# Context values computed in groups of 128 rows and carried to their batches, with two edits at the start of the second attention

## The chip, the core and the metric

The kernel runs as one program on one core of a Trainium2 chip. The core has TensorE (PE in the profile; its weight loads are listed apart as PEld), VectorE (DVE), ScalarE (ACT), GpSimd (POOL) and SyncE (SP). SP does no arithmetic here: it issues transfers, which the DMA engines carry out. The metric is the time of one execution in device microseconds (us). The median of three executions before the change is 1793.78 us (1792.69 to 1799.24).

## The reference, cut to what matters

The reference is a block of four layers on `x` of shape (16, 256, 256), with a context `ctx` of shape (16, 77, 256). Each layer adds a gated result to `x`:

```python
x = x + tanh(g_xattn[0]) * L0_xattn(ctx, layernorm(x), ...)   # attention over context and latents
x = x + tanh(g_ffn[0])   * L0_ffn(layernorm(x), ...)          # 8 experts, the best two of each token
x = x + tanh(g_xattn[1]) * L1_xattn(layernorm(x), ctx, ctx, fside, mask, ...)
x = x + tanh(g_ffn[1])   * L1_ffn(layernorm(x), ...)          # gated linear attention
```

The change is in the third layer and the work that prepares it. That layer is an attention with 16 heads of 16 columns over the 77 context rows of each batch:

```python
q = heads(query @ wq + wq_b); k = heads(ctx @ wk + wk_b); v = heads(ctx @ wv + wv_b)
attn = softmax(q k^T / 4 + mask) * group_prob
out  = merge(attn @ v) @ wo + wo_b
```

Keys and values depend on the context alone, so they can be computed ahead of the layer.

## The kernel before, in words

The kernel works through stages: stage 0 is the first attention, stage 1 the experts, stage 2 the second attention, stage 3 the gated linear attention. Instructions of PE, ACT, DVE and POOL are mostly issued through a wrapper that keeps them in the order of the program on their engine. The profile therefore gives line 50 (the wrapper) for nearly all of them, and one reads by the names of tiles. SP's transfers are not pinned: a scheduler orders them when the program is built, so a load that needs nothing can stand far ahead of the line that asks for it. The built program gives the transfers of SP eight semaphores in turn; a transfer that reuses one first waits for the transfer eight places before it.

Stage 1 (`stage1_fast`) has sixteen blocks of rows: eight experts for each of two halves of the batches. A block is 640 rows. `fetch` loads a block into one of three `xin` buffers, `turned` transposes it on PE by units of up to 256 rows, `expert` multiplies, copies to one of two `y` buffers on DVE, and writes back to `rows_out`. There are 24 units in each half. `route.next_gather` makes POOL gather 128 rows of a half's results and add them to `x` of a batch; there are 32 gathers for each half, and a gather can begin only when the half's writes have landed.

Between the two halves of stage 1 stands the context work, the main object of the change. Until then the context, already transposed, has been loaded by `load` into four tiles `cT0` to `cT3` of four batches each. The loop over the 16 batches calls `context(b)`. For every fourth batch it first computes the keys of four batches (`context_keys`, tile `kd`): PE forms them in two banks of PSUM and ACT copies them out, twice each, with a mask. Then it computes the values of the batch: two products on PE with the 77 context rows as the stationary operand, and one addition of the bias on DVE into the batch's own tile `vc{b}`, where rows lie in partitions 0 to 76. The banks for this come from a shared pool of four that go round in order. From the seventh batch on, the loop also issues ten gathers.

In the second half of stage 1 a table `steps` sets small jobs between the units: normalization of the first batches for the second attention (`prep.stats`, `prep.norm`, `prep.turn`, `prep.queries`), and at unit `half + 20` the job `prep.spread(0)`. `spread(b)` is two POOL copies that put the columns of `vc{b}` into a tile `vd`, even heads in one half and odd heads in the other. There are three `vd` tiles, used in turn.

Stage 2 (`stage2_fast`) takes one batch after another, each in two halves of the heads, c = 0 and 1. `scores` computes scores into a PSUM tile that has a single buffer, then one exponential on ACT makes `e` from all 2048 columns. For c = 0 ACT then copies the batch's `group_prob` tile into a bank (`gpx`). `weigh` multiplies `e` by it on DVE, giving `pg`; for c = 0 in two calls of 1024 columns. `values` multiplies `pg` with `vd`, and `e` with a matrix of ones (`own`) for the denominators, both into the bank `o`. `outputs` divides. PE's order for batch 0 is: scores (0, 0), queries of batch 1, scores (0, 1), values (0, 0), scores (1, 0), and so on. POOL's order in each batch is two gathers, four small operations for a later batch's normalization, one gather, and then `spread` of the next batch.

Beside the results the kernel keeps flags: the exponentials leave their sums in columns of a tile `most`, whose maximum is tested at the end.

Of the kernel before, what the change touches and what calls it, by code (L numbers as in the profile page):

```python
# [17 lines left out]
P = 128  # L18
# [36 lines left out]
def flamingo_kernel(tc: tile.TileContext, t, out):  # L55


    nc = tc.nc
    with tc.tile_pool(name="flag", bufs=1) as fp:
        check = {n: fp.tile(shape, F32, tag=n, name=n) for n, shape in (  # L60
            ("esum", [P, 2 * S]), ("rsum", [P, S]), ("most", [P, 2 * B]), ("uneven", [P, B]),
            ("gates", [P, 2 * B]), ("second", [P, 16]), ("logs", [P, 2 * B]),
            ("rows", [P, 2, 8]), ("rsum2", [P, 2 * B]), ("rsum0", [P, 4 * B]))}
        for x in check.values():
            nc.gpsimd.memset(x, 0.0)
        bad = check["bad"] = fp.tile([1, 1], I32, tag="bad", name="bad")
        layers(tc, t, out, check)
        with tc.If(nc.values_load(bad[0:1, 0:1], min_val=0, max_val=P,
                                  skip_runtime_bounds_check_because="a count of partitions") > 0):
            layers(tc, t, out, None)  # L70
# [3 lines left out]
def layers(ctx: ExitStack, tc: tile.TileContext, t, out, check):  # L74
# [39 lines left out]
    def c_count(j):  # L114
        return min(P, c_rows - P * j)

    def c_pieces(b):

        lo, hi = b * S2, (b + 1) * S2
        return [(j, max(lo, P * j) - P * j, max(lo, P * j) - lo, min(hi, P * j + P) - max(lo, P * j))  # L120
                for j in range(lo // P, (hi - 1) // P + 1)]
# [968 lines left out]
    def stage1_fast(keep, prep, bank):  # L1090
        with ExitStack() as sx:
# [11 lines left out]
            kb = w1.tile([P, 2, 2], F32, tag="kb", name="kb")  # L1103
            dve.tensor_tensor(kb, bc(vec[:, V_KB:V_KB + 2], [P, 2, 2], 2), bc(pmask, [P, 2, 2], 1), ALU.mult)

            mks, cTs = {}, {}

            def load(b):
                mks[b] = w3_.tile([S2, S], I32, tag="mk", name="mk")
                nc.sync.dma_start(out=mks[b], in_=t["maskT"][b])  # L1110
                if b % 4 == 0:
                    cTs[b // 4] = w1.tile([P, 2, 4, S2], F32, tag=f"cT{b // 4}", name=f"cT{b // 4}")
                nc.sync.dma_start(out=cTs[b // 4][:, :, b % 4, :],
                                  in_=t["ctxT"][b].rearrange("(k p) s -> p k s", p=P))

            def mask(b):

# [10 lines left out]

            def context_keys(q):

                cT = cTs[q]
                kds[q] = keep.tile([P, 2, 2, 4 * S2], F32, tag=f"kd{q}", name=f"kd{q}")
                for c in range(2):
                    ps = bank("k")
                    for k in range(2):
                        pe.matmul(ps[:, :4 * S2], wk2[:, k, c * P:(c + 1) * P],
                                  cT[:, k].rearrange("p b s -> p (b s)"), start=k == 0, stop=k == 1)
                    for h in range(2):
                        act.activation(kds[q][:, c, h, :], ps[:, :4 * S2], AF.Identity,
                                       bias=kb[:, c, h:h + 1], scale=pmask[:, h:h + 1])  # L1140

            def context(b):

                if b % 4 == 0:
                    context_keys(b // 4)
                ps, cT = bank("v"), cTs[b // 4][:, :, b % 4, :]
                for k in range(2):
                    pe.matmul(ps[:S2, :D], cT[:, k, :], wv2[:, k, :], start=k == 0, stop=k == 1)
                vc = keep.tile([S2, D], F32, tag=f"vc{b}", name=f"vc{b}")
                dve.tensor_tensor(vc, ps[:S2, :D], bv[:S2], ALU.add)  # L1150
                ctx_side[b] = negs[b], kds[b // 4][:, :, :, b % 4 * S2:(b % 4 + 1) * S2], vc


            tiles = ROWS // P
# [7 lines left out]
            def fetch(x):  # L1162
                xin[x] = w3_.tile([P, tiles, D], F32, tag="xin", name="xin")
                nc.sync.dma_start(out=xin[x], in_=by_expert(route.rows[x // 8], x % 8))
# [36 lines left out]
            def weigh_rows(n):  # L1201
                if n == 0:
# [7 lines left out]
                     12: [(weigh_rows, 2)],  # L1210
                     half + 6: [(prep.stats, 0)], half + 10: [(prep.norm, 0)], half + 11: [(prep.stats, 1)], half + 12: [(add_bias, 0)],
                     half + 13: [(prep.turn, 0)], half + 15: [(prep.norm, 1)], half + 16: [(prep.stats, 2)], half + 18: [(add_bias, 1)],
                     half + 17: [(prep.queries, 0)], half + 19: [(prep.turn, 1)], half + 20: [(prep.spread, 0)]}
            for n in range(4):
                steps.setdefault(2 + n, []).append((route.scatter, last - 1, n))
                steps.setdefault(13 + n, []).append((route.scatter, last, n))
# [19 lines left out]
            fetch(1)  # L1236
            units(0, half)

            for b in range(B):
                context(b)  # L1240
                if b % 4 == 2 and b < 8:
                    fetch(8 + b // 4)
                if b >= 6:
                    route.next_gather()
            units(half, 2 * half)


# [45 lines left out]
    def stage2_fast(prep, bank, begin):  # L1293
        with ExitStack() as sx:
# [13 lines left out]
            def scores(b, c):  # L1308

                neg, kd, _ = ctx_side[b]  # L1310
                qT = prep.qT[b]
                sc = psc.tile([P, 4, 2, S], F32, tag="sc", name="sc")
                for h in range(2):
                    for g in range(4):
                        r = slice(32 * g, 32 * g + 32)
                        pe.matmul(sc[:S2, g, h, :], kd[r, c, h, :], qT[r, c, :], start=True, stop=True)
                e = es[b, c] = w2e.tile([S2, 4, 2, S], F32, tag="e", name="e")
                act.activation(e, sc[:S2], AF.Exp, bias=neg, accum_out=most[:S2, 2 * b + c:2 * b + c + 1])
                if c == 0:

                    gpx[b] = bank("gpx")
                    act.copy(gpx[b][:S2, :S], gps.pop(b))
# [40 lines left out]
            def run(f, b, *a):  # L1363
                if 0 <= b < B:
                    f(b, *a)

            load(0)
            for b in range(B + 1):
                def early(*batches):
                    if b in batches:  # L1370
                        next(begin)

                run(load, b + 1)
                run(scores, b, 0)
                early(B - 1)
                if b > 0:
                    run(prep.turn, b + 1)
                else:
                    prep.queries(1)
                run(values, b - 1, 1)  # L1380
                run(weigh, b, 0, 0, 2)
                run(outputs, b - 1, 1)
                run(weigh, b, 0, 2, 4)
                early(B - 2, B)
                route.next_gather()
                run(scores, b, 1)
                if b > 0:
                    run(prep.queries, b + 1)
                run(prep.norm, b + 2)
                early(B - 1)  # L1390
                run(weigh, b, 1, 0, 4)
                run(project, b - 1)
                early(B - 2, B - 1)
                route.next_gather()
                run(values, b, 0)
                run(outputs, b, 0)
                run(prep.stats, b + 3)
                early(B - 3, B - 1)
                route.next_gather()
                run(prep.spread, b + 1)  # L1400
                if 2 <= b:
                    load_weights(1)
# [883 lines left out]
```

## Time and profile before

The profile shows one execution in detail; its own time is near, but not equal to, the median.

| what | value |
|---|---|
| median of three executions | 1793.78 us (1792.69 to 1799.24) |
| the profiled execution, its time | 1796.44 us |
| the profiled execution, its span | 1794.6 us |
| context work on PE | 981.8 to 1003.9 us from the start of the span |
| one pair of value products on PE | 0.86 us, 16 pairs |
| one addition into `vc` on DVE | 0.42 us, 16 of them |
| second half of the experts | 1003.9 to about 1051.5 us |
| first scores of the second attention | 1051.67 us |
| first product with `vd` | 1058.69 us |
| two copies of `spread` on POOL | 1.11 us |

All times inside the span count from its start. A timeline row gives the start, the duration of a merged group, the engine, the line, the operation with "written tile <- read tiles", and in brackets the idle time before it with what the profile takes to be its cause. A cause named there is inferred; where the named work was long done, it was another. Rows of "SPq" are issues of transfers, not the transfers themselves. A row of stretches gives a window, its length, then the busy time (and number of instructions) of PE, PEld, DVE, ACT and POOL, the clock granted to TensorE as a share, the busy share of the DMA engines and their GB/s.

### The profile page before, as it was taken

What the parts mean: (1) busy time and instruction counts of PE and PEld (TensorE: products, weight loads), DVE (VectorE), ACT (ScalarE), POOL (GpSimd) and SP (SyncE); (2) the same over time, 40 slices, a digit from 0 to 9 for tenths busy, and PEclk for the clock granted to TensorE, in tenths of its full rate; (3) what the DMA queues carried; (4) which work ended last, traced back from release to release, by engine and by line L of the source; (5) the groups of instructions that cost most, each with busy time, mean ns of one, the idle gap of its engine ahead of it and who ended that gap; (6) DMA issues with size and microseconds to landing.
All of it is one profiled execution on the core that took longest, in us unless ns stands there. A gap on an engine that the chain in (4) does not pass through costs nothing.

```text
span 1794.6 us, 35307 instructions
## 1 busy us (share of the span) xinstructions
PE 1764.7 (98%) x13804; PEld 1225.2 (68%) x13804; DVE 1186.2 (66%) x2713; ACT 856.7 (48%) x1762; POOL 1020.6 (57%) x1002
## 2 busy tenths in 40 slices
PE   8999999999999999999999999999999999999998
PEld 5666666667666666667677766666777777777776
DVE  3345665666666666665556348887777778777875
ACT  4433444434434344334443358775456546545643
POOL 3655676576656776576752676612455545545543
PEclk9999999999999999999999999999999999999999
DMA  9800010000100010000027962300112211211211
GB/s 306 239 1 23 13 39 11 28 20 13 32 29 17 15 36 10 29 24 17 13 96 232 284 151 46 51 8 19 35 35 48 41 41 35 52 41 35 44 40 32
DMA packets 121624, 102.30 MB, mean 57 GB/s; under 512 B 53051, under 2 KB 106979, under 8 KB 120937
## 3 DMA queue, kind: packets, MB, share of 16 engines
q1 hardware_dynamic: 109161, 83.17, 16.3%
q0 software_dynamic: 12288, 16.79, 4.7%
q8 instruction: 111, 1.82, 0.4%
q14 instruction: 64, 0.52, 0.1%
HBM read 56.26 MB, written 38.44 MB: 53 GB/s over the span
## 4 chain that ended last, share of the span: by engine, by line
PE 81%; DVE 9%; POOL 7%; issue 1%; DMA 1%; ACT 0%; POOLq 0%; SPq 0%; DVEq 0%; ACTq 0%
PE o L50 12%; PE qk L50 11%; PE v L50 9%; PE sc L50 8%; PE proj L50 8%; PE kq L1641 5%; PE sc L1641 5%; POOL es L50 4%; PE v L1641 3%; PE proj L1641 3%; PE ex L50 3%; PE gq L1641 2%; PE o L1641 2%; DVE at L50 2%; PE q L50 2%; POOL rs L50 2%
## 5 line engine op out<-in xcount | busy, mean ns | idle before, releaser
L50 POOL TENSOR_SCALAR rs<-mv 128x2 f32<-128x2 f32 (+2 forms) x85 | 16.3, 192 | 367.6 <-DVE mv L50 363.9
L50 DVE RECIPROCAL rd<-o 128x256 f32<-128x256 f32 x64 | 112.3, 1755 | 164.0 <-PE o L50 123.6
L50 POOL TENSOR_TENSOR at<-at,at 128x768 f32<-128x768 f32 x63 | 114.3, 1814 | 151.5 <-DVE at L50 151.5
L50 ACT ACTIVATE e<-sc 128x1024 f32<-128x1024 f32 (+1 forms) x192 | 181.7, 1016 | 18.5 <-PE sc L50 18.5
L50 PE MATMUL sc<-qk 64*128 64x256 f32 (+1 forms) x1536 | 183.1, 384 | 0.5 <-DVE qk L50 0.5
L50 PE MATMUL o<-e,v 128*32 128x256 f32 (+1 forms) x3072 | 177.9, 379 | 0.0
L50 PEld LDWEIGHTS sc<-qk 64*128 64x128 f32 (+1 forms) x1536 | 132.0, 172 | 55.1 <-issue 26.8
L50 POOL TENSOR_TENSOR esum<-esum,es 128x512 f32<-128x512 f32 x128 | 163.5, 1277 | 10.0
L50 PE MATMUL qk<-kvT,wkv 128*128 128x333 f32 x512 | 164.3, 443 | 0.0
L50 ACT ACTIVATE qk<-qk 128x256 f32<-128x256 f32 x128 | 48.8, 382 | 231.4 <-PE qk L50 231.4
L50 POOL TENSOR_TENSOR es<-e 128x1024 f32<-128x1024 f32 x64 | 151.3, 2363 | 12.1 <-ACT e L50 9.0
L50 POOL TENSOR_TENSOR es<-es,e 77x1024 f32<-77x1024 f32 x64 | 150.4, 2350 | 5.0
L50 PEld LDWEIGHTS o<-e,v 128*32 128x32 f32 (+1 forms) x3072 | 99.9, 110 | 66.3
L50 PE MATMUL qk<-kvT,wq 128*128 128x256 f32 x512 | 134.6, 385 | 0.0
L50 DVE COPY qk<-qk 128x333 f32<-128x333 f32 x128 | 64.6, 504 | 93.8 <-ACT qk L50 92.8
L50 POOL DMA_INDIRECT x<-rows_out,pos x64 | 101.4, 1584 | 35.9 <-issue 15.7
L50 PEld LDWEIGHTS qk<-kvT,wq 128*128 128x128 f32 x512 | 94.3, 189 | 35.2 <-issue 9.6
L50 PEld LDWEIGHTS qk<-kvT,wkv 128*128 128x128 f32 x512 | 97.2, 190 | 30.0
L50 PE MATMUL proj<-wo0h,oT 128*128 128x256 f32 x512 | 113.7, 380 | 0.3 <-DVE oT L50 0.3
L50 PE MATMUL v<-wkv,kvT 128*128 128x512 f32 x256 | 113.1, 595 | 0.0
L50 PEld LDWEIGHTS proj<-wo0h,oT 128*128 128x128 f32 x512 | 95.9, 190 | 13.9 <-issue 0.8
L50 POOL DMA_INDIRECT rows<-xw,pos x64 | 66.8, 1043 | 58.5 <-DMA rows<-xw,pos 26.6
(258 smaller groups left out, 3927.9 us busy)
## 6 DMA issues: line engine op xcount, KB each, us to landing
rows<-zero SPq DMA_DIRECT2D x16, 640.0 KB
xin<-rows SPq DMA_DIRECT2D x16, 640.0 KB
r<-rms SPq DMA_DIRECT2D x30, 256.0 KB
rows_out<-y SPq DMA_DIRECT2D x16, 384.0 KB
v<-vctx SPq DMA_DIRECT2D x15, 308.0 KB
x<-in_x_dram SPq DMA_DIRECT2D x16, 256.0 KB
rows_out<-y SPq DMA_DIRECT2D x16, 256.0 KB
rows<-picks SPq DMA_DIRECT2D x16, 256.0 KB
```

Of the source, the lines that this page charges most:

```text
L50: x = getattr(self.engine, name)(*a, **k)
L1641: tc.keep_in_program_order(nc.tensor.matmul(*a, **k))
```

## The change

There are three edits.

1. The values of the context are computed for groups of 128 consecutive context rows, without regard to batches. All 16 x 77 = 1232 rows lie in one tile `cT`; there are ten groups, the last of 80 rows. For each group PE makes two products and DVE one addition, into a tile `vg` of a pool of three buffers (the one that also held the mask tiles). `context_rows(j)` then issues transfers on SP that copy the rows of group j to the tiles `vc{b}` of the batches they belong to, into partitions 0 to 76. There are 25 of them, since a group begins and ends in the middle of batches. `context_rows(j - 1)` is called after the products of group j. The gathers of this loop are one in each turn; there are ten as before. Keys are computed as before, ahead of groups 0, 2, 4 and 6.
2. `prep.spread(0)` moves from unit `half + 20` to unit `half + 2`.
3. For batch 0 and c = 0 alone, ACT copies `group_prob` before the exponential, and the exponential is done in two halves of 1024 columns, with the matching half of `weigh` called after each. The calls of `weigh(0, 0, ...)` in the loop of stage 2 go away for batch 0. The flag tile `most` has one more column, for the sum of the second half.

```diff
-            ("esum", [P, 2 * S]), ("rsum", [P, S]), ("most", [P, 2 * B]), ("uneven", [P, B]),
+            ("esum", [P, 2 * S]), ("rsum", [P, S]), ("most", [P, 2 * B + 1]), ("uneven", [P, B]),
...
-                if b % 4 == 0:
-                    cTs[b // 4] = w1.tile([P, 2, 4, S2], F32, tag=f"cT{b // 4}", name=f"cT{b // 4}")
-                nc.sync.dma_start(out=cTs[b // 4][:, :, b % 4, :],
-                                  in_=t["ctxT"][b].rearrange("(k p) s -> p k s", p=P))
+                nc.sync.dma_start(out=cT[:, :, b * S2:(b + 1) * S2], in_=t["ctxT"][b].rearrange("(k p) s -> p k s", p=P))
...
-            def context(b):
-
-                if b % 4 == 0:
-                    context_keys(b // 4)
-                ps, cT = bank("v"), cTs[b // 4][:, :, b % 4, :]
+            def context_values(j):
+                n, ps = c_count(j), bank("v")
                 for k in range(2):
-                    pe.matmul(ps[:S2, :D], cT[:, k, :], wv2[:, k, :], start=k == 0, stop=k == 1)
-                vc = keep.tile([S2, D], F32, tag=f"vc{b}", name=f"vc{b}")
-                dve.tensor_tensor(vc, ps[:S2, :D], bv[:S2], ALU.add)
-                ctx_side[b] = negs[b], kds[b // 4][:, :, :, b % 4 * S2:(b % 4 + 1) * S2], vc
+                    pe.matmul(ps[:n, :D], cT[:, k, j * P:j * P + n], wv2[:, k, :], start=k == 0, stop=k == 1)
+                vcs[j] = w3_.tile([P, D], F32, tag="mk", name="vg")
+                dve.tensor_tensor(vcs[j][:n], ps[:n, :D], bv[:n], ALU.add)
+
+            def context_rows(j):
+                x = vcs.pop(j)
+                for b in range(B):
+                    for i, lo, to, n in c_pieces(b):
+                        if i == j:
+                            if to == 0:
+                                vc = keep.tile([S2, D], F32, tag=f"vc{b}", name=f"vc{b}")
+                                ctx_side[b] = negs[b], kds[b // 4][:, :, :, b % 4 * S2:(b % 4 + 1) * S2], vc
+                            nc.sync.dma_start(out=ctx_side[b][2][to:to + n], in_=x[lo:lo + n])
...
-                     half + 17: [(prep.queries, 0)], half + 19: [(prep.turn, 1)], half + 20: [(prep.spread, 0)]}
+                     half + 17: [(prep.queries, 0)], half + 19: [(prep.turn, 1)], half + 2: [(prep.spread, 0)]}
...
-            for b in range(B):
-                context(b)
-                if b % 4 == 2 and b < 8:
-                    fetch(8 + b // 4)
-                if b >= 6:
-                    route.next_gather()
+            groups = len(c_new)
+            for j in range(groups):
+                if j % 2 == 0 and j < B // 2:
+                    context_keys(j // 2)
+                context_values(j)
+                if j > 0:
+                    context_rows(j - 1)
+                if 2 < j < 5:
+                    fetch(5 + j)
+                route.next_gather()
+            context_rows(groups - 1)
...
+                if b == c == 0:
+                    gpx[b] = bank("gpx")
+                    act.copy(gpx[b][:S2, :S], gps.pop(b))
+                    for n in range(0, 4, 2):
+                        act.activation(e[:, n:n + 2], sc[:S2, n:n + 2], AF.Exp, bias=neg,
+                                       accum_out=most[:S2, n * B:n * B + 1])
+                        weigh(b, c, n, n + 2)
+                    return
...
-                run(weigh, b, 0, 0, 2)
+                if b > 0:
+                    run(weigh, b, 0, 0, 2)
                 run(outputs, b - 1, 1)
-                run(weigh, b, 0, 2, 4)
+                if b > 0:
+                    run(weigh, b, 0, 2, 4)
```

`c_pieces` and `c_count`, which stage 0 already uses in the same way, give for a batch the groups that its rows lie in, with first row, place and number, and the number of rows of a group.

More of the change, by code (lines that the diff above doesn't have):

```diff
@@ L1104, in stage1_fast @@
             dve.tensor_tensor(kb, bc(vec[:, V_KB:V_KB + 2], [P, 2, 2], 2), bc(pmask, [P, 2, 2], 1), ALU.mult)
-            mks, cTs = {}, {}
+            mks, vcs = {}, {}
+            cT = w1.tile([P, 2, B * S2], F32, tag="cT", name="cT")
             def load(b):
@@ L1129, in context_keys @@
             def context_keys(q):
-                cT = cTs[q]
                 kds[q] = keep.tile([P, 2, 2, 4 * S2], F32, tag=f"kd{q}", name=f"kd{q}")
@@ L1136, in context_keys @@
                         pe.matmul(ps[:, :4 * S2], wk2[:, k, c * P:(c + 1) * P],
-                                  cT[:, k].rearrange("p b s -> p (b s)"), start=k == 0, stop=k == 1)
+                                  cT[:, k, 4 * q * S2:4 * (q + 1) * S2], start=k == 0, stop=k == 1)
                     for h in range(2):
```

## The prediction

> **What bounds the kernel now.** I read the page first: whole span, busy shares, chain.
>
> ```profile
> span 1794.6 us, 35307 instructions
> ...
> PE 1764.7 (98%) x13804; PEld 1225.2 (68%) x13804; DVE 1186.2 (66%) x2713; ACT 856.7 (48%) x1762; POOL 1020.6 (57%) x1002
> ...
> PE 81%; DVE 9%; POOL 7%; issue 1%; DMA 1%; ACT 0%; POOLq 0%; SPq 0%; DVEq 0%; ACTq 0%
> ```
>
> TensorE is the bound: work taken from it, or gaps closed on it, shortens the span, unless something new holds it. Only two places are touched, so next comes the timeline there. The context stretch (the second column is the duration of a merged group; "SPq" rows are issues of transfers):
>
> ```profile
> 981.63 2.24 PE L50 MATMUL k<-cT,wk 128*128 128x308 f32 x8
> 983.70 3.62 PE L50 MATMUL v<-wv,cT 128*77 128x256 f32 x16
> 984.77 0.42 DVE L50 TENSOR_TENSOR vc<-v,bv 77x256 f32<-77x256 f32 x1 [2.51 <-PE v L50]
> 986.77 0.43 SPq L890 DMA_DIRECT2D lbk<-in_lbk_dram  x1
> 988.15 0.38 SPq L890 DMA_DIRECT2D we<-in_we_dram  x1
> 994.80 0.34 SPq L890 DMA_DIRECT2D amask<-in_amask_dram  x1
> 994.97 1.63 POOL L50 DMA_INDIRECT x<-rows_out,pos  x1 [14.46 <-DMA lbg<-in_lbg_dram]
> ```
>
> TensorE runs without a gap from 981.8 to 1003.9 (the chain: four times keys 2.07 plus values 3.45). The built program issues a transfer on SP only when the one eight before it has landed, so the issue times give landings: the issue of we3 at 988.15 shows the first row block (x 8, issued 983.46) landed; that of amask at 994.80 shows lbk, issued 986.77, landed 8.0 us after its issue, in order behind 2 MB of row blocks and the rows_out writes.
>
> Then the start of the second attention:
>
> ```profile
> 1053.15 1.96 ACT L50 ACTIVATE e<-sc,neg 77x2048 f32<-77x2048 f32 x1 [4.22 <-DMA halves<-in_halves_dram]
> 1055.11 0.37 ACT L50 COPY gpx<-gp 77x256 f32<-77x256 f32 x1
> 1055.51 2.35 DVE L50 TENSOR_TENSOR pg<-e,gpx 77x1024 f32<-77x1024 f32 x2 [3.99 <-DMA lbg<-in_lbg_dram]
> 1057.77 1.11 POOL L50 COPY vd<-vc 77x128 f32<-77x128 f32 x2
> 1058.69 1.93 PE L50 MATMUL o<-pg,vd 77*32 77x256 f32 x16 [2.33 <-POOL vd L50]
> 1062.26 2.00 PE L50 MATMUL sc<-qT,kd 32*77 32x256 f32 x16
> 1068.59 1.12 POOL L50 COPY vd<-vc 77x128 f32<-77x128 f32 x2
> 1071.53 1.07 PE L50 MATMUL o<-pg,vd 77*32 77x256 f32 x16
> ```
>
> TensorE waits 2.33 us for the exponential, the weighing and vd of batch 0, and then runs slowly: 1.93 for what takes 1.07 later, 2.00 for 1.10. The stretches say why (length, busy time of the five engines, granted clock, DMA share, GB/s):
>
> ```profile
> 1015.00:1019.00 4.00, 4.00 (x23) 3.52 (x22) 1.65 (x5) 1.12 (x2) 1.60 (x2) 1.00 1.05 277
> 1059.00:1063.00 4.00, 4.00 (x40) 1.76 (x36) 1.85 (x1) 1.09 (x4) 3.50 (x4) 0.50 0.49 66
> ```
>
> The clock is 0.50 after the idle time. The other row shows that the transfers are full while the second half of the experts runs (1.00 to 1.14 from 1011 to 1039). Last, SP's own waits (total, times, longest):
>
> ```profile
> SPq L666 <- DMA vctx<-vc: 28.9, 13, 10.1
> SPq L50 <- DMA rms<-rs: 34.5, 15, 3.0
> ```
>
> A small transfer alone lands in 34.5/15 = 2.3 us, but one wait for pieces like those of this change (stage 0 has the same groups, with rows of 4 KB) took 10.1: that for batch 8, whose last piece has 53 rows.
>
> **The change part by part.**
>
> *Values by groups.* 16 pairs of products become 10. A pair takes 3.45/4 = 0.86 us whether the stationary tile has 77 or 128 columns (128-column weights in the expert products run at the same pace, 1.73 for eight instructions against 3.45 for sixteen). TensorE saves 6 x 0.86 = **5.2 us**, all on the chain. DVE's 16 additions of 0.42 become 10; its idle time hides that.
>
> *Carrying.* 25 transfers come onto SP between lbk and row block 11, in the built program mixed with lbg, we3, wq3, wk3; wv3, wo3, dmask, amask move behind row block 11. SP spends about 0.45 us on each, 11 us in all; block 11 was issued at 1007.31 and needed only at 1019.7, so 12 us cover it. The price lies elsewhere: a group's tile comes from a pool of three, so the addition of group 3 waits until the two pieces of group 0 have landed, and so on for each later group. Behind that DVE wait stand the later additions and the first y copies; behind it on TensorE stands the product of group 5, as the four shared banks come round (keys take two, two groups the others).
>
> Group 0 is ready at 985.2; its pieces go out at 987.3 and, waiting for the lane of row block 8, at 988.15, behind lbk. Lower bound of landing: 2.3 us alone, 990.5; then group 3 (ready at 989.4) holds nobody, since group 5 is due only at 981.8 + 3x2.07 + 5x0.86 = 992.3. Upper bound: lbk's 994.8 plus a quarter of 10.1 (rows of 1 KB for 4 KB), 997.3, a stall of 5.4. The landings went in the order of issue, so I take just after lbk, 995.5: addition to 995.9, group 5 at 996.0, **a stall of 3.7 us**. The later waits come while TensorE still has the fourth keys to do, and no other group lacks a bank; the last addition, near 1006, delays y copies that have some 5 us of spare banks.
>
> *Clock after that stall.* The nearest row is the idle 2.33 us that gave 0.50; it cost 2x0.86 + 0.90 + 0.2 = 2.8 us. Bounds 0 and 2.8; this stall is longer, so I take **2.8**. The context stretch then ends 5.2 - 3.7 - 2.8 = 1.3 us later than now (bounds: 5.2 earlier, 3.0 later).
>
> *First spreading sooner.* The two vd copies (with their gap 1.28 us) go between gathers 13 and 14 on POOL; gather 14 waited 0.54 there anyway. vc0 will have landed 20 us before. After that POOL is 0.3 later, and 1.0 earlier once it passes the old place.
>
> *Exponential in halves.* The weight copy (0.37) moves into ACT's idle 4.22; gp was issued at 1046.94, 6 us before; if it came late, the exponential would wait as long. The halves take 1.02 each by the 128x1024 row. Weighing: 1054.3 to 1055.5 and 1055.5 to 1056.7 for 1055.5 to 1057.9. The second scores wait for both halves, 0.15 later than now, 1055.45 to 1056.55. So o starts at 1056.7 instead of 1058.69 and at full clock, as no gap exceeds 0.9. Next: second exponential 1056.65 to 1058.6, scores of batch 1 at 1058.65, weighing of 2.28 to 1061.0, o to 1062.95, scores at 1062.95 instead of 1066.84. **Saved: 3.9 us**; bounds 0.7 (POOL or a late gp holds o to 1058 and the clock drops) and 4.6.
>
> *What is late next.* vd1 on POOL. The gathers start at 994.97 either way and POOL stays at 1.85 us each. With vd0 out of the way and statistics that no longer wait 1.41, vd1 ends about 1067.6 (now 1069.7), while TensorE now wants it at 1071.53 - 3.9 + 1.3 = 1068.9. It just fits; each us that the fuller transfers slow the gathers beyond 1.3 is lost. I deduct 0.3. The wider flag tile costs one column of a fill and of a maximum, nothing.
>
> **Sum:** -5.2 + 3.7 + 2.8 - 3.9 + 0.3 = -2.3 us. From then on TensorE is continuous and the order unchanged, so this reaches the end. The profiled execution took 1796.44 (span 1794.6 and 1.84 around it), 2.7 above the median; 1794.1 for it, **1791.5** as a median.
>
> [...]
>
> **Rivals.**
> - *No stall* (0.2): the small pieces overtake the bulk. For it: they go from one on-chip tile to another; against it: nine landings in order. The stretch ends 5.2 earlier, TensorE then wants vd1 at 1062.4 and gets it at 1067.6: gain 3.9, less up to 2.8 of slow clock. 1790 to 1792.6; 1784.7 only if POOL too were early.
> - *Slower by full transfers* (0.25): 1.26 MB of pieces are new, 4.3 us at the 290 GB/s of that stretch, and 1.38 MB of weights move into it; the spare share there (0.43 and 0.24 of two 4 us rows) is 2.7 us. Rows_out writes then land late, y has two buffers, and the first y copy of a block (1017.9) follows the last write of two blocks before (1010.8) by only 7 us. Price 2 to 7 us on TensorE or on gathers. It decides once the loss passes 2.3: 1794 to 1799. Against it: no y copy waits for a transfer now.
> - *The start doesn't move* (0.05): the first o is held by POOL's gathers or gp; 0.7 saved instead of 3.9, 1794.7.
> - Forecast (0.5): 1789.5 to 1793.5, its own range.
>
> **Numbers.** 8 in 10: 1786.5 to 1799, both bounds of the stall and the full-transfer case. 0.5% is 9 us, about what a measurement of this kernel can tell: faster only if everything is kept (0.04), slower only if stall and full transfers add up (0.09), else within.
>
> **What would show it.** Right: a DVE wait of some 6 us before the fourth vg addition, a TensorE gap of 3 to 4 us before group 5, clock near 0.5 after it; o of batch 0 about 2 us after the second scores' start, at 1.07; vd1 ending just before its o. Wrong: no gap between 992 and 996; y copies or gathers waiting for transfers between 1005 and 1045; TensorE idle at vd1 by over 1 us.

## The result, and the profile after

The changed kernel takes 1803.44 us (median of 8 executions, 1799.03 to 1806.31), the kernel before 1792.67 us beside it (8 executions, 1791.62 to 1799.24). The ratio is 1.0055, 95% interval 1.0041 to 1.0069: about 9.9 us slower (the two medians lie 10.8 us apart). The prediction was 1791.5 us, with 1799.0 as the upper end of its range.

The profiled execution of after took 1803.78 us. Its page, first the span, the busy shares, and the chain by engine:

```profile
span 1802.0 us, 35303 instructions
...
PE 1762.5 (98%) x13780; PEld 1225.4 (68%) x13780; DVE 1184.5 (66%) x2707; ACT 856.6 (48%) x1764; POOL 1020.6 (57%) x1002
...
PE 78%; DVE 9%; POOL 7%; DMA 2%; issue 2%; ACT 1%; SPq 0%; POOLq 0%; DVEq 0%; ACTq 0%
```

TensorE has 2.2 us less to do (1764.7 before), and the span is 7.4 us longer. PE's share of the chain fell from 81% to 78%, and DMA and "issue" gained. Where that is, the timeline of after tells; first TensorE's rows with more than 1 us of idle time before them, in the window 975 to 1085 (start, duration, and in brackets the idle time):

```profile
994.78 1.13 PE L50 MATMUL v<-wv,cT 128*128 128x256 f32 x4 [2.64 <-DVE vg L50]
...
1012.96 1.12 PE L50 MATMUL xT<-ident,xin 128*128 128x128 f32 x4 [4.80 <-DVE y L50]
...
1028.66 2.08 PE L50 MATMUL ex<-ew,xT 128*128 128x256 f32 x4 [3.16 <-ACT xT L50]
```

Only the first of the three stops was foreseen. The two others stand in the second half of the experts, where TensorE had no idle time above 0.3 us before; the one that the timeline of before lists there:

```profile
1005.07 1.99 PE L50 MATMUL ex<-ew,xT 128*128 128x256 f32 x8 [0.29 <-ACT xT L50]
```

SP's rows (issues of transfers) in the same stretch of after:

```profile
985.93 5.07 SPq L1154 DMA_DIRECT2D vc<-vg  x5
992.23 0.35 SPq L890 DMA_DIRECT2D lbg<-in_lbg_dram  x1
993.18 0.39 SPq L890 DMA_DIRECT2D we<-in_we_dram  x1
993.86 3.86 SPq L1154 DMA_DIRECT2D vc<-vg  x5
997.77 0.49 SPq L890 DMA_DIRECT2D wq<-in_wq_dram  x1
998.36 4.01 SPq L1154 DMA_DIRECT2D vc<-vg  x5
1002.41 0.56 SPq L890 DMA_DIRECT2D wk<-in_wk_dram  x1
1003.08 10.75 SPq L1154 DMA_DIRECT2D vc<-vg  x10
1013.93 0.44 SPq L1167 DMA_DIRECT2D xin<-rows  x1
1014.48 0.37 SPq L1192 DMA_DIRECT2D rows_out<-y  x1
```

SP is occupied with the pieces, and four loads of weights among them, from 985.93 to 1013.83. Only then come row block 11 (1013.93; 1007.31 before) and the first written rows of the second half (1014.48; 1007.82 before). The two rows of before:

```profile
1007.31 0.33 SPq L1164 DMA_DIRECT2D xin<-rows  x1
1007.82 3.30 SPq L1189 DMA_DIRECT2D rows_out<-y  x2
```

Inside a merged row like those of after stand gaps, so 10.75 for ten pieces is not 1.07 each; taken one by one the 25 issues last 562 to 955 ns, median 757. Together they take 18.6 of the 27.9 us, the four weights 1.8, and the gaps 7.5. The wait for the transfer eight places before shows in before: of the seven weight loads at the ninth to the fifteenth place from 983.46 on, three waited for xin (3.1 us), three for rows_out (1.4) and one for lbk (0.3).

DVE's rows show who passes the delay on:

```profile
994.30 0.42 DVE L50 TENSOR_TENSOR vg<-v,bv 128x256 f32<-128x256 f32 x1 [5.50 <-DMA vc<-vg]
...
1011.88 0.42 DVE L50 TENSOR_TENSOR vg<-v,bv 80x256 f32<-80x256 f32 x1 [3.04 <-DMA vc<-vg]
1012.22 1.61 DVE L50 COPY y<-ex 128x512 f32<-128x512 f32 x3
...
1026.21 0.69 DVE L50 COPY y<-ex 128x512 f32<-128x512 f32 x1 [4.80 <-DMA rows_out<-y]
```

The last addition waits for pieces until 1011.88, three y copies stand behind it in DVE's order, and TensorE stops for them. At 1026.21 a y copy waits until rows written from the same buffer have landed. Behind it in DVE's order stand the statistics of a normalization, ScalarE waits for these, and the transposed rows that TensorE needs next stand behind that on ScalarE:

```profile
1027.82 0.29 ACT L50 ACTIVATE rs<-mv,eps 128x2 f32<-128x2 f32 x1 [5.75 <-DVE mv L50]
1028.25 0.84 ACT L50 COPY xT<-xT 128x256 f32<-128x256 f32 x2
```

So TensorE's second stop in the experts, 3.16 us at 1028.66, is for written rows that landed late. Row block 11 itself held nobody here: its first transposition, at 1024.90, followed without a wait. The stretches (length, busy time of the five engines, clock, DMA share, GB/s) of after show the slow clock behind the first of the two stops; behind the second the clock is 0.63 from 1027 to 1031 and 0.52 from 1031 to 1035:

```profile
1011.00:1015.00 4.00, 2.04 (x7) 1.87 (x8) 1.95 (x4) 0.59 (x1) 3.39 (x3) 0.50 0.64 108
1015.00:1019.00 4.00, 4.00 (x14) 3.23 (x14) 0.69 (x1) 0.37 (x1) 3.53 (x5) 0.65 1.03 267
```

The start of the second attention in after, against the rows shown of before:

```profile
1064.16 1.11 ACT L50 ACTIVATE e<-sc,neg 77x1024 f32<-77x1024 f32 x1 [2.39 <-DMA halves<-in_halves_dram]
1065.39 2.35 DVE L50 TENSOR_TENSOR pg<-e,gpx 77x1024 f32<-77x1024 f32 x2 [2.54 <-ACT e L50]
1067.54 1.10 PE L50 MATMUL o<-pg,vd 77*32 77x256 f32 x14
...
1077.47 1.13 POOL L50 COPY vd<-vc 77x128 f32<-77x128 f32 x2
...
1078.70 1.07 PE L50 MATMUL o<-pg,vd 77*32 77x256 f32 x16
```

There is no stop at the first o, and the clock stays at 1.00. Every profile of this study is cut at the same four points of TensorE: the first key product, the first transposition of the experts' second half, the first scores of the second attention, and the o of batch 1, c = 0 (1071.53 before, 1078.70 after). From the last point to TensorE's last products it is 715.8 us before and 715.7 after, so the three stretches hold nearly the whole difference:

| stretch on TensorE, us | before | after | predicted difference | measured |
|---|---|---|---|---|
| context | 22.11 | 20.14 | +1.3 | -2.0 |
| second half of the experts | 47.93 | 61.42 | 0 | +13.5 |
| start of the second attention | 19.86 | 15.70 | -3.6 | -4.2 |

The sum, +7.3, is nearly the difference of the spans, 7.4. In the second row the two stops are 8.0 of the 13.5 us; the rest goes with the slow clock behind them. The medians differ by more, for a reason that the last experiments give.

### The profile page after: what moved, and what is told of

Read it like the earlier page. It is cut to its first block, busy times and chain, and to the rows that moved or that the text cites. A ratio compares the mean times of both kernels' runs of the same rounds, so it can differ in the third digit from the quotient of the medians.

```text
span 1802.0 us, 35303 instructions
## 1 busy us (share of the span) xinstructions
PE 1762.5 (98%) x13780; PEld 1225.4 (68%) x13780; DVE 1184.5 (66%) x2707; ACT 856.6 (48%) x1764; POOL 1020.6 (57%) x1002
## 4 chain that ended last, share of the span: by engine, by line
PE 78%; DVE 9%; POOL 7%; DMA 2%; issue 2%; ACT 1%; SPq 0%; POOLq 0%; DVEq 0%; ACTq 0%
PE o L50 12%; PE qk L50 11%; PE sc L50 8%; PE v L50 8%; PE proj L50 8%; PE kq L1659 5%; PE sc L1659 5%; POOL es L50 4%; PE v L1659 3%; PE proj L1659 3%; PE gq L1659 2%; PE o L1659 2%; PE ex L50 2%; DVE at L50 2%; PE q L50 2%
## 5 line engine op out<-in xcount | busy, mean ns | idle before, releaser
L50 PEld LDWEIGHTS proj<-wo0h,oT 128*128 128x128 f32 x512 | 95.9, 190 | 13.9 <-issue 0.8
```

The lines of the kernel that those rows point to most:

```text
L50: x = getattr(self.engine, name)(*a, **k)
```

## The experiments

Two theories at first. A: the pool of three `vg` buffers makes DVE wait for pieces, and y copies stand behind. B: the pieces themselves make everything behind them on SP late, whatever DVE does. Ratios below are to the kernel before, with 95% intervals.

### start_only and groups_only: which edit costs

start_only is the kernel before with the second and third edit; groups_only is after without them.

```diff
-                     ... half + 20: [(prep.spread, 0)]}
+                     ... half + 2: [(prep.spread, 0)]}
```

> The kernel before with the second and third edit alone (spreading at unit half + 2, first exponential in halves); context values by batch, nothing carried by DMA. Both theories (A: the pool of three buffers makes DVE wait; B: the transfers clog the queue) put the loss into the groups, so both expect the start's gain of 4.2 us bare: about 1788.5 us against 1792.7, ratio 0.9977 (0.9970 to 0.9985), with no stop of PE in the second half of the experts. If the two edits have a cost of their own in the experts that the trace of after only hides among the others, the ratio is 0.999 or more.

> The changed kernel without the second and third edit: groups and carrying alone. The whole loss should be here: after's +9.9 us and the 4.2 us that the start gave, so about +14 us, 1806.5 us, ratio 1.0078 (1.006 to 1.0095), with both stops of PE (near 1008 and 1025) as in after. If the early spreading on POOL has a share in the stops, this kernel is at 1.005 or less.

start_only: 0.9987 (0.9978 to 0.9997). groups_only: 1.0052 (1.0033 to 1.0070), against 1.0055 for all three edits. So the loss is in the groups, as expected, but neither number fits the 4.2 us: start_only won 2.3, and beside the groups the two edits won nothing. In the profile of groups_only the start of the second attention takes 15.93 us without them: as the experts end 10 us later there, POOL has the first vd ready anyway. That cure was for a delay that the first edit hides. The context shows the other course that the prediction had named: TensorE's stop there is 4.48 us, the clock is 0.50 behind it, and the stretch takes 24.66 us, 2.55 more than before, where after won 2.0.

### in_place and act_queue: the buffers, and the queue

in_place writes the sums of a group over the columns of `cT` from which the group was made, so no addition waits for a buffer. act_queue issues the pieces on ScalarE.

```diff
-                vcs[j] = w3_.tile([P, D], F32, tag="mk", name="vg")
+                x = vcs[j] = cT[:, :, j * P:j * P + P]      # nine of ten groups
...
-                            nc.sync.dma_start(out=ctx_side[b][2][to:to + n], in_=x[lo:lo + n])
+                            nc.scalar.dma_start(...)            # act_queue
```

> The changed kernel, but DVE writes the values of a group over the context columns that the group was made from (nine of the ten groups), so no addition waits for a buffer to be carried away. The pieces, their number and their queue stay; a row is sent as two runs of 512 bytes. A: the waits of DVE go, and with them the idle time before group 5 (2.6 us), the first stop (4.8 us) and the slow clock behind it (2.8 us): 10 us less than after, near 1792; if the second stop (3.2 and 2.8 us) only followed from the first, 16 us less, near 1786.5. B (the transfers themselves are late for the others, whatever DVE does): within 3 us of after, 1799.5 to 1803, with PE stopping for y and the row blocks as in after.

> The changed kernel with the 25 pieces issued on ScalarE's queue in place of SyncE's; three buffers as in after. Each issue takes a place in ScalarE's order, 19 us in all at the 0.76 us that an issue took on SyncE. A: with three buffers the additions still wait for the pieces, so the first stop stays and the time is 1799 to 1808, more where ScalarE falls behind. B: SyncE's queue is free for rows_out and the row blocks, the second stop goes (6 us), and if the first was lateness of the queue too, the time comes to 1786.5 to 1792.

in_place: 1.0062 (1.0043 to 1.0080), no better than after. The context stretch falls to 16.92 us, the 5.2 us of six pairs exactly, and every wait of DVE for pieces goes. The waits that its profile lists instead (engine and tile, who released it; total, times, longest):

```profile
DVE y L50 <- DMA rows_out<-y: 16.4, 1, 16.4
...
PE xT L50 <- DMA xin<-rows: 7.8, 1, 7.8
```

Its SP rows end like those of after:

```profile
1004.43 7.04 SPq L1159 DMA_DIRECT2D vc<-cT  x8
1011.57 2.51 SPq L1159 DMA_DIRECT2D vc<-vg  x2
1014.18 0.45 SPq L1172 DMA_DIRECT2D xin<-rows  x1
```

The last values are ready near 998, yet their pieces go out at 1011 to 1014, and row block 11 at 1014.18, the first written rows of the half at 1014.73. The experts end at 1062.63, after's at 1063.00. Theory A falls as the cause of the loss: the DVE waits were only the form in which the lateness arrived. act_queue: 1.0079 (1.0061 to 1.0098). The pieces then stand in ScalarE's order, where key copies and transposed rows wait behind them (5.21 us of idle time ahead of keys at 993.13 for kd, 4.51 ahead of expert products at 1017.99 for xT). It moved part of the cost to another place and did not test B cleanly.

So in after SP is held for the most part by the issues themselves, 20.4 of the 27.9 us from 985.93 to 1013.83, and in act_queue the issues given to ScalarE stood ahead of the copies that TensorE then stopped for.

### tiny_pieces and late_block: issues or bytes, and what a late block costs

tiny_pieces is start_only with 25 extra transfers of the same rows but 8 of 256 columns, into a tile that nothing reads. late_block is start_only with block 11's load held by a small write of DVE, which the load overwrites.

```diff
+                for j, lo, to, n in c_pieces(b):
+                    nc.sync.dma_start(out=x25[lo:lo + n, next(x25s)], in_=ctx_side[b][2][to:to + n, :8])
```
```diff
+                if x == 11:
+                    dve.memset(xin[x][:, :, 0:1], 0.0)
...
                     expert(u)
+                    if u == half + 4:
+                        fetch(11)
```

> The kernel with the second and third edit alone (values by batch, straight into place), and beside it 25 transfers of the same numbers of rows as the pieces, but of 8 columns in place of 256, into a tile that nothing reads: extra work with a thirty-second of the bytes. If SyncE's issuing (25 more issues in its order ahead of the next row block) is the price, the next row block is issued some 5 us or more later than in start_only, PE stops for it, and the time is 1796 or more (ratio to before above 1.002). If the bytes or the landing of the pieces are the price, it is as start_only, 0.9987 (0.998 to 1.000).

> The kernel with the second and third edit alone (values by batch, no pieces), with one thing added: the load of row block 11 first waits for a small write of DVE that stands behind the second unit of block 9, near 1013 in place of 1006. It prices the late row block alone, with no piece and no other transfer moved. If lateness of that block is the price, a chain of late written rows and stops of PE follows as in after: ratio 1.001 to 1.006. If there is slack in three buffers (a block takes some 5.5 us, and its load has two blocks of time), it is as start_only, 0.9987.

tiny_pieces: 1.0070 (1.0050 to 1.0090), the whole loss with a thirty-second of the bytes. Its issues last 622 to 1072 ns, median 766, no shorter than those of after. In its SP rows weights and block 11 have moved as in after (in before wo was issued at 993.22):

```profile
1006.04 0.53 SPq L890 DMA_DIRECT2D wo<-in_wo_dram  x1
1006.68 5.03 SPq L1245 DMA_DIRECT2D x<-vc  x6
...
1012.83 0.37 SPq L1164 DMA_DIRECT2D xin<-rows  x1
```

Yet it isn't block 11 that TensorE stops for, as was expected: it waits 0.72 us for it, at 1019.03. The long stop is that of after's second one, for written rows, which were first issued at 1013.30 (1006.93 in start_only). DVE's row and TensorE's:

```profile
1021.29 0.69 DVE L50 COPY y<-ex 128x512 f32<-128x512 f32 x1 [6.64 <-DMA rows_out<-y]
```
```profile
1023.74 1.91 PE L50 MATMUL ex<-ew,xT 128*128 128x256 f32 x4 [4.09 <-ACT xT L50]
```

In this profile 6.6 us of the loss are in the experts (54.51 against 47.93 in start_only) and 2.2 at the start of the second attention, where pg waits 4.22 us for rows_out; that wait is not in after.

late_block: 1.0018 (1.0008 to 1.0029), with no piece at all; that is 0.31% or 5.6 us above start_only. Its experts take 52.39 us instead of 47.93. A further 1.9 us of its profile lie far behind, after the last of the four points: an idle time of 1.46 us near 1230, which start_only has too, is followed there by 3.41 us of half clock. From its timeline, the load (merged with the next one) and the product that waited for it:

```profile
1013.00 1.88 SPq L1166 DMA_DIRECT2D xin<-rows  x2
```
```profile
1022.16 0.93 PE L50 MATMUL xT<-ident,xin 128*128 128x128 f32 x4 [2.96 <-DMA xin<-rows]
```

So this row block took 9.2 us from its issue to its use. Of the 12.4 us between issue (1007.31) and need (1019.7) that the prediction counted as cover, 3.2 were free by this row; a delay of 6.6 leaves 3.4, and the stop is 2.96, with the slow clock behind it. In other runs where TensorE waited for the block it took less: 6.2 us in tiny_pieces, 7.1 in weights_late, 7.2 in in_place. So 3 to 6 of the 12.4 us were free. And late_block's stretch is only 4.5 us longer, where after's is 13.5: in after TensorE stopped for y copies behind DVE's wait for pieces, and for late written rows. No run prices these two apart.

### Where the pieces can stand: by_units, in_stage2, weights_late, pieces_held

All four compute in place. by_units sets the pieces between the units of the second half and keeps SP's transfers of that stage in program order; in_stage2 keeps `cT` through the second attention and carries one batch per batch there; pieces_held is in_stage2 with its buffers in a pool of that stage; weights_late is in_place with the weights of the fourth layer held until the second attention.

```diff
+            for b in range(1, B):                                   # by_units
+                steps.setdefault(half + 3 + b, []).append((context_rows, b))
...
+                if b + 3 < B:                                       # in_stage2
+                    carry(b + 3)
...
+                if 4 <= b + 3 < B:                                  # pieces_held
+                    carry(b + 3, w1)
...
         for x, src in weights[:n]:                                 # weights_late
+            if fast:
+                dve.memset(x[:, 0:1], 0.0)
             nc.sync.dma_start(out=x, in_=src)
```

> In place as in in_place, but SyncE's row blocks, written rows and pieces of the experts' stage keep the order of the program, and the pieces of one batch are issued per unit of the second half, from its fifth unit on (the first batch's in the context loop). The weights of the fourth layer that nothing holds are then issued earlier, in the first half. If the place of the pieces ahead of the next row block is the price, no row block waits behind pieces, and the values' 5.2 us and the start's 2 to 4 us are both won: ratio 0.995 to 0.9965 to before (1784 to 1788). If the added bytes are the price wherever they go in the experts' stage (DMA share there near 1 before), stops come back at other places and the ratio is 1.000 or more.

> In place as in in_place, with the context columns kept until the end of the second attention: only the pieces of batches 0 to 3 are issued in the experts' stage, the others one batch per batch of the second attention, three batches ahead, into four buffers that are used in turn. Both readings (order on SyncE, or bytes in the experts' stage) expect most of the loss to go: 7 pieces in place of 25 ahead of the row block. Ratio 0.9945 to 0.997 to before (1783 to 1789), the values' 5.2 us and the start's 2 to 4 us; if the second attention is short of DMA or SyncE, its batches grow and the ratio is 0.998 or more.

> As pieces_in_stage2, but the three buffers that take batches 4 to 15 belong to the second attention, so no piece for them can be issued before the experts end, and SyncE does not stand at one. Six pieces (batches 0 to 3) stay ahead of the fourth row block of the half. If the order on SyncE was the price, that block is issued near 1007, PE does not stop in the experts' stage, and the values' 5.2 us and the start's 2 to 4 us are won: ratio 0.995 to 0.997 to before. If carrying costs elsewhere (the second attention's batches grow), 0.998 or more.

> In place as in in_place, all 25 pieces in the context's place, but the weights of the fourth layer (2.9 MB) are held until the second attention by a small write of DVE ahead of each. If 25 issues by themselves hold the row block back, it is issued near 1012 and the ratio is 1.002 to 1.006 as before; if it was pieces and weights together on one queue (backlog), pieces are through by 1004, the block is issued near 1007, and the ratio is 0.995 to 0.997.

by_units: 1.0058 (1.0038 to 1.0078). Inconclusive: the fixed order put SP behind waits for y (13.9 us at one of them), so block loads were late again, and the context began 4 to 6 us later than elsewhere (985.98) as weights had moved into the first half.

in_stage2: 1.0098 (1.0081 to 1.0115). My own mistake, and a clear lesson: the scheduler hoisted the pieces of batch 4 ahead of block 11, and they wait for a buffer that POOL reads late. SP's own waits in that profile:

```profile
SPq L1155 <- POOL vd L50: 21.0, 1, 21.0
```

Block 11 went out at 1020.56 and TensorE stood 15.79 us.

weights_late: 1.0016 (1.0008 to 1.0025). Without the big weights between them the 25 pieces end at 1008.5, block 11 goes out at 1008.59, and the experts end at 1053.63, 9.0 us earlier than in in_place for a block issued 5.6 us earlier. Neither of the two issue times that were expected (near 1012, or near 1007) came, but one between them. So weights pushed behind the row block (in after wv and wo at 1014.90 and 1018.98) cost something too; how much is not priced apart. The experts still take 56.32 us, 8.4 more than in start_only: the context ends 4.9 us sooner, so a block issued at 1008.59 is late for TensorE (a stop of 2.30 us), and a y copy waits 8.45 us for written rows (a stop of 4.32).

pieces_held: 1.0012 (1.0001 to 1.0022). Block 11 is issued at 1001.14 and the first scores come at 1047.66, 4.0 us earlier than before; the experts take 50.09 us, with one stop of 2.35 left. But after the first scores TensorE stops 6.38 us. The first group_prob tile is now loaded only at 1049.49, behind the last written rows, since its place in this layout comes free later, and ACT waits 9.33 us for it. That is the experiment's side effect and not the change's.

### held_gp, held_gp_weights, and the pools in another order

held_gp gives that tile a place of its own; held_gp_weights adds the late weights; m1 and m2 are these two with the pool of xin opened ahead of the pool of y.

```diff
+            self.gp0 = keep.tile([S2, S], F32, tag="gp0", name="gp0")   # held_gp
...
-            w2 = sx.enter_context(tc.tile_pool(name="f1w2", bufs=2, reuse_waits="tile"))   # m1, m2
             w3_ = sx.enter_context(tc.tile_pool(name="f1w3", bufs=3, reuse_waits="tile"))
+            w2 = sx.enter_context(tc.tile_pool(name="f1w2", bufs=2, reuse_waits="tile"))
```

> As pieces_held, with the first batch's group_prob tile in a place of its own, so that its load does not wait for the experts' last y copy; batches 0 to 2 keep their buffers, 3 to 15 take three in turn. The 6.4 us stop at the start of the second attention and the slow clock behind it (together 9 us against start_only) go; nothing else changes. If the row block's issue time on SyncE is what the change lost, the experts end near 1047 and the ratio is 0.9945 to 0.9970 to before (1783.5 to 1788). If the second attention pays for the pieces it now carries, 0.998 or more.

> As held_gp, with the weights of the fourth layer held until the second attention as in weights_late. If the 2.3 us stop that pieces_held still had in the experts came from weights that were issued at 995 to 998 and share the wires with row blocks issued from 1001, it goes: 2 to 4 us below held_gp, ratio 0.993 to 0.996. If weights in the second attention are late for the fourth layer (weights_late took 1.3 us more from its first scores to the end than start_only), the gain is cancelled: within 0.1% of held_gp.

> As held_gp, with one thing moved: in the experts' stage the pool of xin is opened ahead of that of y, so the second attention's first e tile lies over xin and not over y, whose last rows must have landed before e is written (ACT waited 5.9 us there in held_gp, PE 2.9, and the clock fell). If that was all that was left, the start takes 15.7 us in place of 20.4: 4.5 us below held_gp, ratio 0.9960 to 0.9980. If some other wait stands next at the same place, no change: 0.999 to 1.000.

> As held_gp_weights with the same change of the pools: 3 to 4.5 us below held_gp_weights, ratio 0.9955 to 0.9975; without an effect 0.998 to 1.000.

| kernel | ratio | context | experts | start |
|---|---|---|---|---|
| held_gp | 0.9994 (0.9983 to 1.0005) | 16.93 | 47.83 | 20.36 |
| held_gp_weights | 0.9990 (0.9981 to 1.0000) | 16.93 | 47.84 | 18.64 |
| m1 (held_gp, pools) | 1.0005 (0.9992 to 1.0017) | 16.93 | 47.84 | 21.33 |
| m2 (held_gp_weights, pools) | 0.9999 (0.9988 to 1.0010) | 16.92 | 47.84 | 25.67 |

In all four only four pieces stand ahead of the row block and of the written rows behind it. The block is issued near 1001, the experts take their 47.8 us again, and the first scores come 5.3 to 6.1 us earlier than in start_only. From held_gp:

```profile
1001.24 0.33 SPq L1167 DMA_DIRECT2D xin<-rows  x1
```
```profile
1045.50 1.10 PE L50 MATMUL sc<-qT,kd 32*77 32x256 f32 x16 [0.52 <-DVE y L50]
```

That confirms the cause. But none is faster than before beyond its interval: the start takes 2.8 to 9.8 us longer in these profiles than start_only's 15.86. (held_gp_weights was profiled in its fastest execution, 1787.97 us, where its median is 1791.61.) In held_gp ACT's first e waited 5.93 us for rows_out, since e lay over y; in m1, pg does. DVE's rows of m1:

```profile
1044.60 0.42 DVE L50 COPY y<-ex 128x256 f32<-128x256 f32 x1 [0.17 <-PE ex L50]
1050.92 4.55 DVE L50 TENSOR_TENSOR pg<-e,gpx 77x1024 f32<-77x1024 f32 x3 [5.90 <-DMA rows_out<-y]
```

The last written rows land 4 to 6 us after the last y copy, and in both held_gp and m1 an early tile of the second attention lies over y. In the two other kernels a wait of about the same length stands at the same place, and the profile puts it down to something else (5.72 us of ACT for q, 5.68 of DVE for lbg), so there it is argued only. Whether a layout without this would keep the 5.2 us was not tried.

### before_again: is the profiled execution typical?

The kernel before, unchanged, profiled twice more.

> The kernel before, unchanged, for another profile. The prediction took the 2.33 us stop for vd and the slow clock behind it from one profiled execution, of 1796.4 us, while half of the executions of this kernel take 1790.8 to 1792.5. If the stop belongs to every execution, this profile has 19 to 20 us from the first scores to the third product with vd, as that one had (19.86). If it comes and goes, a profile of an execution near 1791 shows 15.5 to 17 us, and the start's gain of 4 us was the price of a stall that the median execution does not have.

> The same once more: 19 to 20 us from the first scores to the third product with vd if the stop is in every execution, 15.5 to 17 us in an execution near 1791 if it comes and goes.

The first took 1791.62 us, the second 1795.13. The first o of each, and the clock of the 4 us from 1059; first execution:

```profile
1056.47 1.07 PE L50 MATMUL o<-pg,vd 77*32 77x256 f32 x16 [2.17 <-POOL vd L50]
```
```profile
1059.00:1063.00 4.00, 4.00 (x62) 2.06 (x54) 3.29 (x8) 3.86 (x9) 3.54 (x4) 1.00 0.55 70
```

Second execution:

```profile
1057.07 1.94 PE L50 MATMUL o<-pg,vd 77*32 77x256 f32 x16 [2.86 <-POOL vd L50]
```
```profile
1059.00:1063.00 4.00, 4.00 (x34) 1.71 (x27) 1.20 (x4) 1.18 (x4) 3.23 (x3) 0.50 0.47 66
```

The stop for vd is in both, the slow clock in one. The start takes 16.58 and 20.40 us. Context, experts and the rest are the same to 0.1 us in both, so what lies between the two executions is this one stretch. start_only takes 15.86: against the first it wins 0.7 us, against the second 4.5. This fits its ratio, 2.3 us (0.5 to 3.9) and not 4.2, and that after loses 9.9 us by the ratio and 7.3 by the profiles: the profiled execution of before was one of those with the slow clock.

## Why the prediction was wrong, point by point

- **Values by groups, 5.2 us: right.** In in_place the context takes 16.92 us against 22.11.
- **Stall before group 5, 3.7 (0 to 5.4): right in kind, 2.64 in after.** The addition of group 3 waited 5.50 us, where some 6 were named. **Slow clock after it, 2.8: did not come in after.** The clock stayed at 1.00. In groups_only it did come, behind a stop of 4.48, so the smaller context of after is in part luck.
- **Carrying on SP: the step that failed.** "SP spends about 0.45 us on each, 11 us in all; block 11 was issued at 1007.31 and needed only at 1019.7, so 12 us cover it." Three sizes in it were wrong. An issue took 0.76, not 0.45. With gaps, waits and weights between them the pieces held SP for 27.9 us, not 11. And the cover was 3 to 6 us, not 12: a load took 6.2 to 9.2 us from issue to use. Beside the sizes the step looked at the row block alone. The half's written rows stand behind the pieces too (1014.48 in place of 1007.82), and it is for these that TensorE made its second stop in after; its first stop was for y copies behind an addition that waited for pieces. tiny_pieces shows that the issues alone suffice; late_block shows that a late load alone costs 4.5 us in the experts; held_gp shows that the experts are whole again when SP is free in time.
- **"The last addition, near 1006, delays y copies that have some 5 us of spare banks": wrong for the same reason.** It came at 1011.88. But in_place, without this wait, ends the experts at the same time.
- **The rival "slower by full transfers" named the right end and the wrong price.** It had the late rows_out and the two y buffers, and the second stop of after passes through them; but it priced bytes, 2 to 7 us, and tiny_pieces shows that the number of issues suffices. So its range, like mine, ended at 1799.
- **Exponential in halves, 3.9: right against the profiled execution (4.2 with the vd step, vd1 ending 0.1 us before its o), too large for the median** (2.3 us in start_only), because it was measured on one execution whose stop had a slow clock behind it. I noted that it lay 2.7 us above the median and still carried its stall to the median in full. Beside the groups the edits won nothing (groups_only).

## What to carry to other kernels

An engine that does no arithmetic can be the bound, as SP was here with 27.9 us of pieces and weights ahead of a load: before adding transfers to a queue, multiply their number by an issue time taken from the same kind of transfer, and compare the result with the slack of everything that stands behind them on the queue: of the next load, counted to its landing and not to its issue, and of the next write, whose landing gives a buffer back. The profile of before had transfers between on-chip tiles in the fourth layer: 15 of `low` were issued in 596 ns (median), 16 of `lowd` in 536. At these times the 25 issues come to 13 to 15 us, where 11 was predicted; they took 18.6. A stall with a slow clock behind it, found in one profile, is worth its full price only if the median execution has it; compare the profiled time with the spread first. And a transfer that a scheduler may hoist can hold the whole queue at a buffer that comes free late (21.0 us in in_stage2).

The one version here whose interval lies below 1 is start_only, the change without its groups: 0.9987 (0.9978 to 0.9997).

## What the runs showed of the hardware that I had not expected

- **The issue of a piece from one on-chip tile to another takes about 0.8 us here, with 32 bytes a row as with 1 KB.** The median is 757 ns in after, 766 with 8 of 256 columns, and 811 for those of held_gp_weights that go out between 1103 and 1161, where SP has little else. The group_prob load of 77 rows of 1 KB from memory was issued in 300 ns at 1068.75 there, a block of 640 rows takes 320, and the pieces of stage 0, which go from the chip to memory, 298 (median) in the profile of before.
- **About equal idle times of TensorE lower the clock or not.** 2.17 (before_again), 2.64 (after) and 2.67 (held_gp_weights) left it at 1.00; 2.33 (before), 2.54 (m1) and 2.86 (before_again) halved it, for 6.83 us each by the clock records of the traces. The idle time of 1.45 us near 1230 lowered it for 3.41 us in late_block, weights_late, m2 and by_units, and not in before, start_only, after and held_gp. So a stop of this length is a chance here and not a fixed price. By the same records the slow spells lasted 3.41 (late_block), 6.83 (after, before), 10.24 (pieces_held) and 17.07 us (m2). Why an idle time of about the same length brings one in one execution and none in another, no run shows.
